# The score constant of each row as VectorE dot products, and y in two banks of 512

## The chip, the core and the metric

The kernel runs on one core of a Trainium2 chip. A core has five engines, each with a queue of its own that it works through in order: TensorE (PE in the profile; PEld is its loading of weights), VectorE (DVE), ScalarE (ACT), GpSimd (POOL) and SyncE (SP), which here issues transfers only. They wait for each other by semaphores. TensorE writes to eight accumulator banks (PSUM), which VectorE or ScalarE must empty. The metric is the device time of one execution in microseconds (us), the median of several runs.

## The reference, cut to what matters

```python
# x: (2708, 1024) f32, adj: (2708, 2708) of 0 and 1, sparse, the early rows dense
q, k, v = x @ W_q.T + b_q, x @ W_k.T + b_k, x @ W_v.T + b_v
z = (q @ k.T) / sqrt(1024) * adj
z = where(z == 0, -10000, z)
x = layernorm(x + relu(softmax(z, axis=1) @ v))      # layer 0
x = layernorm(x + adj @ (x @ weight) + bias)          # layer 1
```

Only the scores of a row's few neighbours matter. With M = W_q.T W_k and two vectors u and w (from the weights and biases), the score of row i and neighbour j is

```
z[i, j] = (y[i] . x[j]) / 32 + c[i],   y[i] = x[i] M + w,   c[i] = x[i] . u + (b_q . b_k) / 32
```

So the kernel computes y (1024 numbers a row) and the constant c (one number a row) once, keeps them in memory as one row of 1028, and gathers rows of y and x for each score. This change is about where c is computed.

## The kernel before, in words

The 2708 rows are 22 blocks of 128 (the last has 20). Rows are sorted by number of neighbours within two families, blocks 0 to 7 and blocks 8 to 21, so that each sorted block has a fixed number of neighbour slots (SLOTS, line 32).

*Start (to about 140 us).* The weights are loaded and turned, M is built (L608) and kept in four tiles m_sb of 1028 columns: 1024 of M, the column u (L601) and three of zeros. Beside it, `list_columns` reads the adjacency block by block and VectorE lists the neighbours (L222 to L229).

*y blocks.* `y_block(b)` (L289) multiplies a block of x, laid out as 8 tiles xt, with m_sb. Its 1028 columns are cut in three (y_cuts, L97: 342, 343, 343), each in one of the four banks of the pool p_o (L119), each over 8 products of 128 (L319). VectorE adds the bias row y_bc and moves each third to a tile yo (L323), with high priority in the schedule; SyncE stores yo (L328) to one of two arrays y_ds, one for each family. ScalarE sums the columns of xt meanwhile (`column_sums`, L332), for the mean row of x. Blocks 0 to 7 run in a loop of their own (L628), beside the rest of the listing, the dealing out of the densest rows (`deal_hub`) and the two sorts; `records_back(f)` (L585) turns the sorted records of a family, which GpSimd has scattered to memory and read back (tabs, L568), into degrees and masks; its first instruction is the copy at L593.

*Attention.* `attend(b)` (L788) gathers y for a sorted block (gather_y, L680, GpSimd's indirect transfers), gathers x rows for each slot into one of nine tiles g that are used in rotation (G1 = 9, L663; cleared once by GpSimd, L670), scores them on VectorE (L774), takes the softmax and adds up the weighted rows to r (L829 on ScalarE, L831 on VectorE). `attend_shares` does the same for block 0 and the hub rows (L908). A finished r is turned on TensorE (`flip`, L698) and multiplied with W_v (`project`, L721, two banks of p_o); VectorE empties these at L867.

*Order around the change.* A list written by hand, `steps` (L1042), says in which order y blocks 8 to 21, single projections ("v") and paired projections ("p") go to TensorE; a running credit (L1068) decides how many attention jobs are put beside each step. From this program order a scheduler makes the order of each engine's queue. Blocks 6 to 0 attend beside the second family's y; their y rows are of the first family. All other blocks gather y of the second family, so they begin when that is stored. What an instruction waits for holds up all that stands behind it on its engine.

*End.* After the paired projections of layer 0 (L958 in their shared code), layer 1 gathers sums of normalised rows and multiplies them with the second weight.

Of the kernel before, what the change touches and what calls it, by code (L numbers as in the profile page):

```python
# [9 lines left out]
F32 = mybir.dt.float32  # L10
# [5 lines left out]
ALU = mybir.AluOpType  # L16
# [4 lines left out]
P = 128  # L21
# [3 lines left out]
HALF = 512  # L25
# [17 lines left out]
ROW, DEG, OFF = 24, 25, 26  # L43
# [37 lines left out]
def sparse_part(ctx, tc, x, xT, adj, wqT, wkT, wvT, bq, bk, bv, w1, b1, out):  # L81
    nc = tc.nc
    N, D = x.shape
    DC = D // P
    NH = D // HALF
    scale = 1.0 / math.sqrt(D)
    NB = (N + P - 1) // P
# [6 lines left out]
    KW = HUB_KEYS + HUB_SLOTS + 5  # L94
    J0 = SLOTS[0]
    YW = D + 4
    y_cuts = [(YW * i // 3, YW * (i + 1) // 3) for i in range(3)]  # L97
    URGENT = 2000
    last = [b for b in range(NB) if SLOTS[b] == 0]
    single = [b for b in range(NB) if SLOTS[b] == 1]  # L100
# [11 lines left out]
    with es:  # L112
# [176 lines left out]
        def y_block(b):  # L289
            r0, n = b * P, rows[b]  # L290
            xt = xts[b]
            if b == NB - 1:
                column_sums(b)

                nc.vector.tensor_reduce(xbT, xs, AX.X, ALU.add)
                nc.vector.tensor_scalar_mul(xbT, xbT, 1.0 / N)
            yo = yos[b % 2]
            y_d, o0 = y_ds[b >= FAMILY], r0 - FAMILY * P * (b >= FAMILY)
            if b == NB - 1:

                assert n <= HUB
                po = p_o.tile([P, HALF], F32, name="po")
                with tc.high_priority(URGENT):
                    for c in range(DC):
                        for g in range(G):
                            nc.tensor.matmul(po[g * HUB:(g + 1) * HUB, :YW // G], xt[:, c, :HUB],
                                             m_sb[c // 2][:, c % 2, g * YW // G:(g + 1) * YW // G], start=(c == 0), stop=(c == DC - 1))
                    for g in range(G):
                        gs, cs = slice(g * HUB, g * HUB + n), slice(g * YW // G, (g + 1) * YW // G)
                        nc.vector.tensor_add(yo[gs, cs], po[gs, :YW // G], y_bc[gs, cs])  # L310
                for g in range(G):
                    gs, cs = slice(g * HUB, g * HUB + n), slice(g * YW // G, (g + 1) * YW // G)
                    nc.sync.dma_start(out=y_d[o0:o0 + n, cs], in_=yo[gs, cs])
                return
            firsts = []
            for h, (k0, k1) in enumerate(y_cuts):
                po = p_o.tile([P, HALF], F32, name="po")
                for c in range(DC):
                    put = nc.tensor.matmul(po[:, :k1 - k0], xt[:, c, :], m_sb[c // 2][:, c % 2, k0:k1], start=(c == 0), stop=(c == DC - 1))  # L319
                    if c == 0:  # L320
                        firsts.append(put)
                with tc.high_priority(URGENT):
                    nc.vector.tensor_add(yo[:n, k0:k1], po[:n, :k1 - k0], y_bc[:n, k0:k1])  # L323
            products.append(put)
            if b < NB - 1:
                column_sums(b, firsts)
            load_x()
            nc.sync.dma_start(out=y_d[o0:o0 + n], in_=yo[:n])  # L328

        def column_sums(b, behind=None):  # L330
            for c in range(DC):
                put = nc.scalar.activation(junka, xts[b][:, c, :], AF.Copy, accum_out=xs[:, c, b:b + 1])  # L332
                if behind is not None and c % 3 == 0:
                    follow(put, behind[c // 3])

        def follow(later, earlier, same=False):

            kind = mybir.DependencyClass.NoSync if same else mybir.DependencyClass.Sync
            tc.add_manual_dep(later.ins, earlier.ins.name, mybir.DependencyInfo(kind, mybir.DependencyReason.DATA),
                              reason="an engine's queue shall not stand still for a transfer")  # L340
# [241 lines left out]
            nc.vector.tensor_scalar(less_, ok, FAR, -FAR, op0=ALU.mult, op1=ALU.add)  # L582
            return put

        def records_back(f):  # L585
            b0, nb = families[f]
            bs, js = slice(b0, b0 + nb), slice(0, max(SLOTS[max(b0, 1):b0 + nb]))
            if f == 0:
                deg0 = lists.tile([P, 1], F32, name="deg0")
                follow(nc.vector.tensor_copy(deg0, tab0[:, DEG:DEG + 1]), products[-1])  # L590
                nc.vector.tensor_scalar_add(deg0[:HUB], deg0[:HUB], float(-J0))
                masks(valid0, less0, deg0)
            follow(nc.vector.tensor_copy(degs[:, bs], tabs[:, bs, DEG]), products[-1])  # L593
            masks(valid[:, bs, js], less[:, bs, js], degs[:, bs])


# [21 lines left out]
                    sorted_.append(0)  # L618
        y_bc = xa.tile([P, YW], F32, name="y_bc", bufs=1)
        bcast_rows(y_bc, y_col)  # L620
        mm = p_mm.tile([P, HALF], F32, name="mm")
        nc.tensor.matmul(mm[:, :1], ones, bqk, start=True, stop=True)
        nc.vector.memset(y_bc[:, D:], 0.0)
# [4 lines left out]
        for b in range(FAMILY):  # L628
# [17 lines left out]
                sort_end(1)  # L646
            if b == 0:
                records_back(0)
        records_back(1)
        wb.release()  # L650
        la.release()
        lists.release()
# [10 lines left out]
        def g_tile():  # L663

            return gp.tile([P, D], F32, name="g", tag="g")

        with tc.high_priority(URGENT):

            for _ in range(G1):
                nc.gpsimd.memset(g_tile(), 0.0)  # L670

        def gather(src, b, word, n):
            return gather_slot(src, tabs[:n, b, word:word + 1], n, g_tile())
# [348 lines left out]
        def finish_pair(pair, ts):  # L1022
            for k, (b, t) in enumerate(zip(pair, ts)):
                xr, sums = pair_x[b], [stat.tile([P, 1], F32, name=f"sm{h}", bufs=6) for h in range(NH)]
                for h in (0, 1) if k == 0 else (1, 0):
# [13 lines left out]
        late_jobs = [7, 20, 8, 19, 18, 8, 17, 8, 16, 11, 15, 10, 20, 9, 14, 19, 13, 12, 18]  # L1039
        late = set(late_jobs)  # L1040
        jobs, late_jobs = jobs + late_jobs, len(late_jobs)
        steps = [("y", 8), ("y", 9), ("y", 10), ("y", 11), ("v", 6), ("y", 12), ("v", 5), ("y", 13), ("v", 4), ("y", 14), ("v", 3),  # L1042
                 ("y", 15), ("v", 2), ("y", 16), ("y", 17), ("y", 18), ("y", 19), ("y", 20), ("y", 21)]
        steps += [("v", b) for b in [1, 0] + last] + [("p", pair) for pair in pairs]

        def blocks_of(step):
# [25 lines left out]
        for i, (kind, b) in enumerate(steps):  # L1072
            if pending is not None:
                pending[0](*pending[1:])
                credit -= END * (2 if pending[0] is finish_pair else 1)
                pending = None
            credit += STEP if kind != "p" else 2 * STEP - P_END
            step[0] = i
            for entry in joining[:]:
                if i >= entry[1] + 2:  # L1080
                    entry[1] = i
                    next(running[entry[0]])
                    if entry[0] in got:
                        joining.remove(entry)
            if kind == "p" and b == pairs[0]:

                (q11, q12), (q21, q22) = wv_q
                wv_t = differences()
                nc.vector.tensor_sub(q12, q12, q11)
                nc.vector.tensor_sub(wv_t[0], q22, q12)  # L1090
                nc.vector.tensor_sub(wv_t[1], wv_t[0], q11)
                nc.vector.tensor_sub(wv_t[2], q21, wv_t[0])
            for c in [c for st in steps[i:i + 3] for c in blocks_of(st) if not (left_y and c in late)]:
                while c not in done0 and c not in got and c != 0:
                    credit -= run_job()
            while 0 in jobs and i >= 15:
                credit -= run_job()
            while jobs and credit > 0 and len([c for c in got if c not in done0 and c not in ALONE and c != "hub"]) < (RB - 1 if left_y else RB):
                if left_y and len(jobs) <= late_jobs:
                    break  # L1100
                credit -= run_job()
            for k, c in steps[i:i + 2]:
                if k != "y" and c not in turned and not (left_y and k == "p"):
                    turned[c] = turn0(c) if k == "v" else turn_pair([lambda rT, r=got[b_]: flip(r, rT) for b_ in c], xb_pools[0])
                    done0.update(blocks_of((k, c)))
            if kind == "y":
                y_block(b)
                credit -= Y_END
                left_y -= 1
                if left_y == 0:  # L1110
                    xa.release()
                    xb_pool = tc.alloc_tile_pool(name="xb", bufs=1, side="right", reuse_waits="tile")
                    xb_pools.append(xb_pool)
                    xb_bc.append(xb_pool.tile([P, D], F32, name="xb_bc"))
                    bcast_rows(xb_bc[0], xbT)
            elif kind == "v":
                xr = gather_x(x, b)
                pending = finish0, b, (project_mean if b in last else project)(turned[b], wv_q), xr
            else:
                for b_ in b:  # L1120
                    pair_x[b_] = gather_x(x, b_)
                pending = finish_pair, b, project_pair(b, *turned[b])
# [460 lines left out]
```

## Time and profile before

The median is 1090.86 us of three runs (1090.35 to 1092.21).

| | busy us | share of the span |
|---|---|---|
| TensorE | 1015.2 | 93% |
| TensorE weight loads | 540.1 | 50% |
| VectorE | 826.3 | 76% |
| ScalarE | 428.1 | 39% |
| GpSimd | 486.7 | 45% |

| groups that the change touches | busy us | count | mean ns |
|---|---|---|---|
| L319 TensorE, y products of 342 and 343 columns | 296.3 | 1008 | 454 |
| L323 VectorE, evictions of y | 31.8 | 63 | 507 |
| L774 VectorE, scores of gathered rows (1024 wide) | 133.1 | 109 | 1221 |
| L721 TensorE, single projections (512 columns) | 101.7 | 224 | 611 |
| L867 VectorE, evictions of these | 10.8 | 16 | 683 |

How to read it: each f32 product of 128x128 is two records in the trace, so a y block of 24 products is 48. TensorE's records overlap: a mean of 454 ns is the time from the start of one to its own end, while the next starts earlier; the pace is read from start to start. Busy shares are over the whole span; what an engine costs in one stage has to be read from that stage.

### The profile page before, as it was taken

The page shows a single profiled execution, that of the slowest core. Times are in us where ns is not written, and L with a number is a line of the kernel's source. Part 1 is how long each engine was busy: PE and PEld are TensorE (multiplying, and loading weights), DVE is VectorE, ACT ScalarE, POOL GpSimd, SP SyncE. Part 2 cuts the span into 40 slices and gives each one's busy share as a digit, 9 for nine tenths or more (in the row PEclk, how much of TensorE's full clock was granted, in tenths as well). Part 3 has the DMA queues.
Part 4 walks back from the last instruction along what each step waited for, and adds up shares of the span by engine and source line. Part 5 has one row for each costly group of instructions (what it writes and reads, how often), then busy time and mean ns, then how long its engine had stood idle before and what let it go on. Part 6 is the DMA issues. An engine that isn't in the chain of part 4 may idle for free.

```text
span 1091.0 us, 10751 instructions
## 1 busy us (share of the span) xinstructions
PE 1015.2 (93%) x3177; PEld 540.1 (50%) x3177; DVE 826.3 (76%) x1801; ACT 428.1 (39%) x896; POOL 486.7 (45%) x397
## 2 busy tenths in 40 slices
PE   7999999999798989999998999999589999999993
PEld 6444466556454545466644444444244444445441
DVE  8799999980487789965297999984477777896431
ACT  4688697412131323232333253342512363324322
POOL 1000230067453546623066476631477777887300
PEclk9999999999999999999999899999799999999997
DMA  9555468435786746635142487835598689979601
GB/s 363 193 211 202 164 219 292 137 95 153 259 261 209 236 160 222 212 126 187 43 124 97 140 275 261 280 125 183 159 302 245 207 241 320 297 221 321 180 39 41
DMA packets 85219, 218.22 MB, mean 200 GB/s; under 512 B 15354, under 2 KB 37338, under 8 KB 82444
## 3 DMA queue, kind: packets, MB, share of 16 engines
q0 software_dynamic: 48768, 148.05, 42.3%
q1 hardware_dynamic: 36384, 69.40, 18.8%
q8 instruction: 27, 0.44, 0.2%
q14 instruction: 40, 0.33, 0.1%
HBM read 208.60 MB, written 33.68 MB: 222 GB/s over the span
## 4 chain that ended last, share of the span: by engine, by line
DVE 32%; PE 28%; issue 18%; DMA 10%; POOL 7%; ACT 3%; POOLq 0%; DVEq 0%; ACTq 0%
PE po L958 17%; PE po L319 6%; DVE few L225 6%; DVE a L222 5%; DVE junkv L774 5%; DMA g<-in_x_dram,tabs 4%; DVE r L831 3%; PE po L721 2%; POOL g L349 2%; DVE t L970 1%; POOL tab_d L563 1%; DMA g<-x_d,tabs 1%; DMA yg<-y_d,tabs 1%; PE tr L247 1%; POOL xr L343 1%
## 5 line engine op out<-in xcount | busy, mean ns | idle before, releaser
L319 PE MATMUL po<-m_sb,xt 128*128 128x343 f32 (+1 forms) x1008 | 296.3, 454 | 11.5 <-DVE yo L323 6.3
L319 PEld LDWEIGHTS po<-m_sb,xt 128*128 128x128 f32 x1008 | 190.4, 190 | 111.9 <-DVE yo L323 8.0
L774 DVE SCALAR_TENSOR_TENSOR junkv<-yg,g 128x1024 uint8<-128x1024 f32 x109 | 133.1, 1221 | 28.5 <-DMA g<-in_x_dram,tabs 16.2
L349 POOL DMA_INDIRECT g<-in_x_dram,tabs x86 | 114.3, 1330 | 76.4 <-ACT r L829 25.2
L958 PE MATMUL po<-t,s_all 128*128 128x512 f32 x272 | 126.6, 609 | 10.6 <-DVE t L970 6.5
L1191 DVE SCALAR_TENSOR_TENSOR r<-g,valid,r 128x1024 f32<-128x1024 f32 x77 | 98.6, 1281 | 17.8 <-DMA g<-x_d,tabs 17.2
L608 PE MATMUL po<-wk_o,wq_o 128*128 128x512 f32 x256 | 110.5, 592 | 0.0
L721 PE MATMUL po<-wv,rT 128*128 128x512 f32 x224 | 101.7, 611 | 6.2 <-DVE yo L323 2.8
L757 ACT ACTIVATE junks<-t,lnm 128x1024 uint8<-128x1024 f32 (+1 forms) x43 | 49.3, 1147 | 120.8 <-DVE lnm L755 103.9
L332 ACT ACTIVATE junka<-xt 128x128 f32<-128x128 f32 x176 | 53.9, 307 | 100.7 <-PE po L319 62.1
L958 PEld LDWEIGHTS po<-t,s_all 128*128 128x128 f32 x272 | 52.6, 196 | 78.2 <-issue 61.1
L958 PE MATMUL po<-w,rT 128*128 128x512 f32 x192 | 87.9, 607 | 0.0
L349 POOL DMA_INDIRECT g<-x_d,tabs x67 | 77.0, 1149 | 22.7 <-issue 16.5
L831 DVE SCALAR_TENSOR_TENSOR r<-g,pr,r 128x1024 f32<-128x1024 f32 x64 | 82.0, 1281 | 6.3 <-ACT r L843 4.8
L563 POOL DMA_INDIRECT tab_d<-rec,pos_i x22 | 25.1, 1141 | 129.9 <-DVE pos_i L552 123.5
L770 ACT ACTIVATE t<-t,nmr,rstd 128x1024 f32<-128x1024 f32 (+1 forms) x43 | 52.5, 1237 | 70.7 <-DVE nmr L769 64.2
L225 DVE MAX8 few<-a 128x8 f32<-128x75 f32 (+3 forms) x132 | 78.8, 616 | 0.0
L608 PEld LDWEIGHTS po<-wk_o,wq_o 128*128 128x128 f32 x256 | 48.4, 190 | 59.3 <-issue 59.0
L721 PEld LDWEIGHTS po<-wv,rT 128*128 128x128 f32 x224 | 43.2, 195 | 60.0 <-issue 53.5
L958 PE MATMUL po<-w,s_all 128*128 128x512 f32 x160 | 72.1, 592 | 0.0
L222 DVE SCALAR_TENSOR_TENSOR a<-a,iota 128x2708 f32<-128x2708 f32 (+1 forms) x22 | 65.2, 2963 | 5.4 <-ACT junk L221 5.4
L220 ACT ACTIVATE junk<-a 128x2708 uint8<-128x2708 f32 (+1 forms) x22 | 54.1, 2458 | 26.9 <-DMA a<-in_adj_dram 22.3
(332 smaller groups left out, 1475.4 us busy)
## 6 DMA issues: line engine op xcount, KB each, us to landing
a<-in_adj_dram SPq DMA_DIRECT2D x21, 1354.0 KB, 5.7
y_d<-yo SPq DMA_DIRECT2D x21, 514.0 KB, 5.4
xt<-in_xT_dram SPq DMA_DIRECT2D x21, 512.0 KB, 5.6
wq_i<-in_wqT_dram SPq DMA_DIRECT2D x8, 512.0 KB, 10.0
wk_i<-in_wkT_dram SPq DMA_DIRECT2D x8, 512.0 KB, 10.2
wv<-in_wvT_dram SPq DMA_DIRECT2D x16, 256.0 KB, 6.8
w<-in_w_dram SPq DMA_DIRECT2D x4, 1024.0 KB, 6.5
g<-in_x_dram,tabs POOLq DMA_INDIRECT x86, 5.6
```

The costliest lines, as they stand in the source:

```text
L220: nc.scalar.activation(junk[:n], a[:n], AF.Sign, accum_out=cnt[:n, b:b + 1])
L222: nc.vector.scalar_tensor_tensor(a[:n], a[:n], 1.0, iota[:n], op0=ALU.is_equal, op1=ALU.mult)
L225: nc.vector.max(few[:n, i * 8:(i + 1) * 8], a[:n, cuts[i]:cuts[i + 1]])
L319: put = nc.tensor.matmul(po[:, :k1 - k0], xt[:, c, :], m_sb[c // 2][:, c % 2, k0:k1], start=(c == 0), stop=(c == DC - 1))
L332: put = nc.scalar.activation(junka, xts[b][:, c, :], AF.Copy, accum_out=xs[:, c, b:b + 1])
L349: nc.gpsimd.indirect_dma_start(out=dst[:n], out_offset=None, in_=src, in_offset=bass.IndirectOffsetOnAxis(ap=at, axis=0), bounds_check=N - ...
L608: nc.tensor.matmul(po, wq_o[i // 2][:, o, i % 2 * P:(i % 2 + 1) * P], wk_o[:, o, hs], start=(o == 0), stop=(o == DC - 1))
L721: put = nc.tensor.matmul(acc, rT[:, c, :], w[c // 4][h][:, c % 4, :], start=(c == 0), stop=(c == DC - 1))
L774: nc.vector.scalar_tensor_tensor(junkv[:n], yg[:n, :D], scale, xg[:n], op0=ALU.mult, op1=ALU.mult, accum_out=s)
L831: nc.vector.scalar_tensor_tensor(r[:n], xg[j][:n], pr[:n, j:j + 1], r[:n], op0=ALU.mult, op1=ALU.add)
L958: put = nc.tensor.matmul(acc, a[:, k], w[:, k], start=start and k == 0, stop=stop and k == DC // 2 - 1, skip_group_check=True)
L1191: nc.vector.scalar_tensor_tensor(r[:n], xg[:n], ok[:n, j:j + 1], r[:n], op0=ALU.mult, op1=ALU.add)
```

## The change

The constant c leaves the product. y_block multiplies only the 1024 columns of M, in two banks of 512, and stores the first 1024 numbers of each row. The vector u is spread over all partitions once (u_bc). A new function, `row_constants(f)`, loads each block of x rows of a family into a g tile and takes the dot product with u_bc on VectorE, one instruction of 1024 a block, adds (b_q . b_k)/32, and stores four numbers a row (c and three zeros) into columns 1024 to 1027 of y_ds[f]. It is called for the first family after its y blocks, ahead of records_back(1), which is now ordered behind it on VectorE, and for the second family ahead of y block 17. The small block 21 keeps its old form, c included. In `steps`, each y block from 12 on moves ahead of the projection that it followed. column_sums is tied to four matmuls of a block instead of three.

The purpose is that a y block takes two accumulator banks of the four instead of three, and that the product has whole banks.

```diff
-    y_cuts = [(YW * i // 3, YW * (i + 1) // 3) for i in range(3)]
...
-            for h, (k0, k1) in enumerate(y_cuts):
+            for h in range(NH):
+                k0, k1 = h * HALF, (h + 1) * HALF
                 po = p_o.tile([P, HALF], F32, name="po")
                 for c in range(DC):
-                    put = nc.tensor.matmul(po[:, :k1 - k0], xt[:, c, :], m_sb[c // 2][:, c % 2, k0:k1], start=(c == 0), stop=(c == DC - 1))
-                    if c == 0:
+                    put = nc.tensor.matmul(po, xt[:, c, :], m_sb[c // 2][:, c % 2, k0:k1], start=(c == 0), stop=(c == DC - 1))
+                    if c % (DC // 2) == 0:
                         firsts.append(put)
                 with tc.high_priority(URGENT):
-                    nc.vector.tensor_add(yo[:n, k0:k1], po[:n, :k1 - k0], y_bc[:n, k0:k1])
+                    nc.vector.tensor_add(yo[:n, k0:k1], po[:n], y_bc[:n, k0:k1])
...
-            nc.sync.dma_start(out=y_d[o0:o0 + n], in_=yo[:n])
+            nc.sync.dma_start(out=y_d[o0:o0 + n, :D], in_=yo[:n, :D])
...
-                if behind is not None and c % 3 == 0:
-                    follow(put, behind[c // 3])
+                if behind is not None and c % 2 == 0:
+                    follow(put, behind[c // 2])
...
-        def records_back(f):
+        def records_back(f, behind=None):
...
-            follow(nc.vector.tensor_copy(degs[:, bs], tabs[:, bs, DEG]), products[-1])
+            put = nc.vector.tensor_copy(degs[:, bs], tabs[:, bs, DEG])
+            follow(put, products[-1] if behind is None else behind, same=behind is not None)
...
+        u_bc = xa.tile([P, D], F32, name="u_bc", bufs=1)
+        bcast_rows(u_bc, u_col)
...
-        records_back(1)
...
+        c_all = stat.tile([P, NB - 1, YW - D], F32, name="c_all", bufs=1)
+        nc.vector.memset(c_all, 0.0)
+        def row_constants(f):
+            b0, end = families[f][0], min(sum(families[f]), NB - 1)
+            for b in range(b0, end):
+                xg = g_tile()
+                nc.sync.dma_start(out=xg, in_=x[b * P:(b + 1) * P])
+                nc.vector.scalar_tensor_tensor(junkv, xg, 1.0, u_bc, op0=ALU.mult, op1=ALU.mult, accum_out=c_all[:, b, 0:1])
+            put = nc.vector.tensor_scalar(c_all[:, b0:end, 0], c_all[:, b0:end, 0], y_bc[:, D:D + 1], None, op0=ALU.add)
+            nc.sync.dma_start(out=y_ds[f][:(end - b0) * P, D:].rearrange("(b p) e -> p b e", p=P), in_=c_all[:, b0:end])
+            return put
+
+        put = row_constants(0)
+        records_back(1, put)
...
-        steps = [("y", 8), ("y", 9), ("y", 10), ("y", 11), ("v", 6), ("y", 12), ("v", 5), ("y", 13), ("v", 4), ("y", 14), ("v", 3),
-                 ("y", 15), ("v", 2), ("y", 16), ("y", 17), ("y", 18), ("y", 19), ("y", 20), ("y", 21)]
+        steps = [("y", 8), ("y", 9), ("y", 10), ("y", 11), ("y", 12), ("v", 6), ("y", 13), ("v", 5), ("y", 14), ("v", 4), ("y", 15), ("v", 3),
+                 ("y", 16), ("v", 2), ("y", 17), ("y", 18), ("y", 19), ("y", 20), ("y", 21)]
...
             if kind == "y":
+                if b == NB - 5:
+                    row_constants(1)
                 y_block(b)
```

## The prediction

> **What bounds the kernel now.** I read first the busy time per stage, then TensorE's idle stretches inside the stage that the change touches, then what VectorE did in those stretches. The stages are: the y blocks of the first family beside the listing of the adjacency (140 to 276.6 us), the y blocks of the second family beside the attention of blocks 6 to 0 (276.6 to 466.7), y blocks alone (to 540.3), the late attention jobs with the paired projections (to 730). Columns after the stretch: its length, then the busy time of TensorE, its weight loads, VectorE, ScalarE, GpSimd, then granted clock, DMA share, GB/s.
>
> ```profile
> 140.00:276.60 136.60, 132.39 (x466) 86.37 (x463) 103.56 (x309) 66.65 (x183) 50.39 (x54) 1.00 0.59 184
> 276.60:466.70 190.10, 172.41 (x522) 96.76 (x522) 157.27 (x281) 48.62 (x171) 97.53 (x75) 0.97 0.67 221
> 466.70:540.30 73.60, 73.60 (x312) 47.88 (x311) 34.73 (x72) 23.67 (x110) 15.58 (x13) 1.00 0.36 116
> 540.30:730.00 189.70, 182.08 (x596) 88.83 (x594) 173.88 (x371) 73.65 (x138) 109.16 (x77) 0.98 0.56 184
> ```
>
> TensorE is idle for 17.7 us of the second stretch and for nothing of the third, where VectorE has 39 us free. So the y stage ends when TensorE has done its work plus those 17.7 us. The idle stretches, and two rows that give the pace (start, duration, then idle before and its releaser in brackets):
>
> ```profile
> 280.86 11.19 PE L319 MATMUL po<-m_sb,xt 128*128 128x343 f32 x32 [4.23 <-DVE yo L323]
> 293.88 14.48 PE L319 MATMUL po<-m_sb,xt 128*128 128x342 f32 x48 [1.84 <-DVE nms L801]
> 320.50 4.88 PE L319 MATMUL po<-m_sb,xt 128*128 128x343 f32 x16 [2.03 <-DVE yo L323]
> 335.07 8.83 PE L721 MATMUL po<-wv,rT 128*128 128x512 f32 x16 [2.83 <-DVE yo L323]
> 385.78 4.88 PE L319 MATMUL po<-m_sb,xt 128*128 128x343 f32 x16 [3.29 <-DVE t L867]
> 451.16 15.67 PE L721 MATMUL po<-wv,rT 128*128 128x512 f32 x32 [2.56 <-DVE nm L892]
> ...
> 358.51 13.90 PE L721 MATMUL po<-wv,rT 128*128 128x512 f32 x32
> 372.24 1.04 PE L698 MATMUL tr<-ident,r 128*128 128x128 f32 x8
> ...
> 480.60 27.82 PE L319 MATMUL po<-m_sb,xt 128*128 128x342 f32 x96
> 508.26 0.28 PE L926 MATMUL mm<-den,tops 128*128 128x1 f32 x2
> ```
>
> Six waits, 16.8 us, all for VectorE to empty one of the four accumulator banks (the other 0.8 us waits for a transposed r). It is late not for lack of speed but of order: the eviction stands in its queue behind an instruction that waits for a transfer. The first case:
>
> ```profile
> 279.31 0.20 DVE L593 CAST degs<-tabs 128x14 f32<-128x14 int32 x1 [20.56 <-DMA tabs<-tab_d]
> 280.31 0.92 DVE L323 TENSOR_TENSOR yo<-po,y_bc 128x342 f32<-128x342 f32 x2
> 288.23 1.23 DVE L774 SCALAR_TENSOR_TENSOR junkv<-yg,g 128x1024 uint8<-128x1024 f32 x1 [7.00 <-DMA yg<-y_d,tabs]
> ```
>
> The attended rows r are not the limit: r of block 5 is done at 311.5 and turned on TensorE at 343.7. What follows the y stage does wait for it:
>
> ```profile
> POOL yg L343 <- DMA y_d<-yo: 35.7, 1, 35.7
> ```
>
> GpSimd stands for 35.7 us until the second family's y is stored, so the late jobs start when the y stage ends.
>
> **What the Trainium skill says.** "PSUM — Partial Sum Buffer", The four PSUM rules: a matmul's output fits one bank of 512 fp32. The trace has 343-column products, each taking a bank alone, and 512-column ones at L721; four banks hold 1371 columns of y now and 2048 after. "TensorE: Matmul & The Clock Gate", Back-to-back issue gap: the gap grows with the columns, plus about 2.5 ns. The trace agrees: 27.66 us / 96 = 288.1 ns for 342.7 columns, 13.73 / 32 = 429.1 ns for 512; that is 0.833 ns a column and a remainder of 2.6 ns. "Perfetto Trace Analysis", Per-engine timelines: ScalarE, VectorE and GpSimd are strict FIFO; the L593 line shows it. "DMA: Bandwidth & Descriptors", Anatomy of one DMA: about 2 us fixed, then bytes at 436 GB/s; that would be 3.2 us (estimate) for a 512 KB x tile, while the page of this kernel has 5.6 us for the 512 KB xt loads, and I use 5.6.
>
> **The change part by part.**
> *TensorE work.* A y block was 48 records of 288.1 ns = 13.83 us, and becomes 32 of 429.1 = 13.73: 0.10 us a block, 2.1 over 21. Eight transposes for u_bc add 1.0 (eight took 1.04 us at L191). Net 1 us: the narrower matrix is not what the change is worth.
> *VectorE work.* An eviction of 343 holds the engine 0.42 us to the next start, one of 512 0.60: 1.26 against 1.20 a block, nothing. Added are 21 dots of 1024; the like-formed L774 takes 1.25 from start to start: 26 us.
> *First family's dots (8).* They stand behind the found rows (250.5 us) and ahead of L593, in a stretch where VectorE is 0.66 us busy of 20 (260 to 280). The loads go out behind the store of y block 5 (229 us) as the g buffers are cleared (222 to 231); at 200 to 300 GB/s, 4.2 MB land by 245 to 252. Dots and c are done by about 263, c stored by 268, while yg is gathered at 281 because GpSimd issues one gather each 1.27 us until then. Hidden: 0. GpSimd has two x gathers fewer ahead of the last scatter, whose landing the read-back of tabs waits for (1.3 us each): L593 goes at 276.7 instead of 279.3.
> *Two banks instead of three.* Four banks were 18.4 us of lead for y blocks, now 27.5; with projections (two banks) alternating, about 22 becomes 27.5. Also y block 12 moves ahead of projection 6. I walk TensorE through the built kernel's own order. Block 7 ends at 258 as before; blocks 8 and 9 fill the banks until 285.7, after L593: the 4.23 us are gone. Bank 2 of block 8 is evicted after four scoring dots (288 + 6 = 294), so 10.2 waits 1.5 us, and blocks 11.1 and 11.2 some 2 us each in the same way: block 11 ends at 319. Then five times turn, y, projection at 0.87 + 13.73 + 13.73 = 28.33: 460.7. VectorE's evictions keep their places in its stream: projection 6 at 357, 5 at 385, 4 at 419, 3 at 450, where TensorE has these at 347, 376, 404, 432, never more than four banks ahead. So no further wait to 460.7, against 466.7 before, and y block 16 is inside it. Left are 17 to 20 and the small 21: 4 x 13.73 + 4 = 59: 519.7 if nothing holds it.
> *Second family's dots (13).* They stand between the evictions of 16.1 and 17.2, and add 16.3 us to VectorE's stream. The place that 16.2 takes in it came at 465.5 before (then bank 3 of block 15); with the dots and the adds of block 0 between, I count on from there and get 16.2 at 468, 17.1 at 489, 17.2 at 497, 18.1 at 505, 18.2 at 512. Block 20's banks are those of 18, so this is now as late as TensorE: end at 523. New waits come on top. Dots 5 to 9 load into g buffers that block 0's second piece reads only some 3 to 4 us earlier in the stream, against 5.6 to land: some 5 us. Nine tiles one after the other at 250 GB/s take 2.1 us each: some 2 more. The queue of SyncE has the store of c behind all dots, and behind that the xt of block 20: about 503 + 5.6 = 509, within the same delay. Bounds: 0 (all hidden) to 20 us (each of the nine late loads seen in full, 9 x 2.2). I take 5: the y stage ends at 528 instead of 540.2, 12.2 earlier.
> *After it.* The mean x (L295) now stands behind the last y eviction, where it was 1.3 us before the end; its path to the first L831 took 8.6 us (538.9 to 547.6), and 3 such adds came before the first scoring dot, while yg was in flight. I lose 2.5 of the gain. The rest (VectorE 92% busy to 730, then layer 1) shifts whole.
> Sum: 1090.9 - 12.2 + 2.5 = 1081.
>
> **The rivals.** *All hidden*: dot loads land in time and the mean costs nothing; end of y at 523, time 1090.9 - 17.5 = 1073. For it: 39 us of free VectorE in the third stretch. Against: the buffers reused within 4 us. *VectorE takes TensorE's place*: the delay is near 17 us, y ends at 540, and with the lost 2.5 the time is 1091 to 1093. For it: one queue for dots, evictions and block 0's adds. *Slower*: block 0's last piece has its gathers behind the dots' buffers, and the xt of block 20 behind c's store; 25 us of delay end y at 545 and give 1090.9 + 5 + 2.5 = 1098. Against: the DMA share there is 0.36.
>
> **How the numbers follow.** Forecast 0.52, all hidden 0.21, VectorE in place 0.14, slower 0.13. The range leaves out the slow case and the best of the hidden one: 1071 to 1092. Faster by over 0.2% (below 1088.7): the first two and a little of the third, 0.77; same 0.07; slower 0.16.
>
> **What would show it.** TensorE idle from 276 to 467 falls from 17.7 to under 8 us, with none before 285; L593 waits to about 277. Second-family dots (L682 there) show waits for their x loads of 3 to 8 us in all; y ends near 528. The first yg gather stays near 281. It is wrong if the c store or block 20's xt ends the stage, if an x load delays tabs, or if later stages take the shift back.

## The result, and the profile after

The changed kernel takes 1079.47 us (median of 4 runs, 1078.66 to 1080.41) against 1091.53 (4 runs, 1090.35 to 1093.06) for the kernel before: ratio 0.9889, 95% interval 0.9872 to 0.9906. On another chip it came out at 0.9889 again. The forecast of 1081 holds; its reason holds only in part, as the experiments show.

The busy time per stretch of the kernel after, columns as in the prediction (length, TensorE, its weight loads, VectorE, ScalarE, GpSimd, granted clock, DMA share, GB/s):

```profile
276.60:466.70 190.10, 183.98 (x456) 82.64 (x455) 157.73 (x271) 54.46 (x201) 94.60 (x72) 1.00 0.72 237
466.70:530.00 63.30, 61.47 (x239) 30.77 (x237) 45.66 (x94) 22.52 (x93) 23.54 (x19) 1.00 0.67 225
```

TensorE is idle for 6.1 us of the first stretch (17.7 before), and its granted clock there is 1.00 (0.97 before). TensorE's idle stretches in the kernel after, up to the end of the y stage (start, duration, form, then idle before and its releaser):

```profile
293.19 7.13 PE L319 MATMUL po<-m_sb,xt 128*128 128x512 f32 x16 [1.26 <-DVE yo L323]
301.28 7.13 PE L319 MATMUL po<-m_sb,xt 128*128 128x512 f32 x16 [0.95 <-DVE yo L323]
308.88 7.13 PE L319 MATMUL po<-m_sb,xt 128*128 128x512 f32 x16 [0.47 <-DVE yo L323]
317.54 14.14 PE L319 MATMUL po<-m_sb,xt 128*128 128x512 f32 x32 [0.65 <-DVE yo L323]
334.47 13.97 PE L739 MATMUL po<-wv,rT 128*128 128x512 f32 x32 [2.79 <-DVE pr L834]
...
512.42 3.67 PE L305 MATMUL po<-m_sb,xt 128*32 128x257 f32 x64 [1.29 <-DMA xt<-in_xT_dram]
```

The waits at 281, 386 and 451 us that the prediction showed have no successor. The VectorE lines that answer to the prediction's: the read-back of tabs, the first scoring dot, the only second-family dot that waited, and the last eviction of the y stage:

```profile
273.83 0.17 DVE L593 CAST degs<-tabs 128x14 f32<-128x14 int32 x1 [12.08 <-DMA tabs<-tab_d]
287.30 1.23 DVE L792 SCALAR_TENSOR_TENSOR junkv<-yg,g 128x1024 uint8<-128x1024 f32 x1 [11.84 <-DMA yg<-y_d,tabs]
471.62 1.22 DVE L682 SCALAR_TENSOR_TENSOR junkv<-g,u_bc 128x1024 uint8<-128x1024 f32 x1 [0.20 <-DMA g<-in_x_dram]
522.33 0.69 DVE L323 TENSOR_TENSOR yo<-po,y_bc 128x512 f32<-128x512 f32 x1 [4.38 <-PE po L319]
```

The y stage ends at 523.0 us (522.33 + 0.69) instead of 540.8: 17.8 us earlier. The profiled spans differ by 14.1 us only (1091.0 to 1076.9). So 3.7 us are given back later; the last experiments' section says where.

The 17.8 us are: 10.2 less of TensorE waits from y block 8 to the end of the y stage (17.6 to 7.4), 5.1 less lost to a halved clock there (5.1 to 0; summed as length times one minus the granted clock, in slices of 5 us), 1.3 less work (13 blocks at 0.10), and 0.6 by an earlier start of y block 8 (257.4 instead of 258.0). That leaves 0.6 unexplained. The clock term is not in the forecast at all, and part of it is luck: in a second profile of the same kernel it was 1.7 instead of 0.

### The profile page after: what moved, and what is told of

Its sections match the earlier page's. It is cut to its first block, busy times and chain, and to the rows that moved or that the text cites. A ratio compares the mean times of both kernels' runs of the same rounds, so it can differ in the third digit from the quotient of the medians.

```text
span 1076.9 us, 10217 instructions
## 1 busy us (share of the span) xinstructions
PE 1007.8 (94%) x2849; PEld 475.1 (44%) x2849; DVE 847.2 (79%) x1825; ACT 428.4 (40%) x898; POOL 490.7 (46%) x397
## 4 chain that ended last, share of the span: by engine, by line
PE 18%; issue 12%; DVE 11%; DMA 4%; POOL 3%; ACT 2%; POOLq 0%; DVEq 0%; ACTq 0%
PE po L976 16%; DVE junkv L792 2%; DVE r L849 2%; DMA g<-x_d,tabs 2%; DVE r L1211 1%; DMA yg<-y_d,tabs 1%; ACT junks L775 1%; DVE t L988 1%; POOL xr L343 1%; PE tr L716 1%; POOL g L349 1%; POOL x_d L703 1%; PE po L739 1%; PE tr L729 1%; POOL r L349 1%
## 5 line engine op out<-in xcount | busy, mean ns | idle before, releaser
L319 PE MATMUL po<-m_sb,xt 128*128 128x512 f32 x672 | 292.2, 594 | 3.3 <-DVE yo L323 3.3
L319 PEld LDWEIGHTS po<-m_sb,xt 128*128 128x128 f32 x672 | 126.4, 190 | 159.6 <-issue 150.8
L739 PE MATMUL po<-wv,rT 128*128 128x512 f32 x224 | 97.7, 594 | 3.3 <-DVE pr L834 2.8
```

The costliest lines, as they stand in the source:

```text
L319: put = nc.tensor.matmul(po, xt[:, c, :], m_sb[c // 2][:, c % 2, k0:k1], start=(c == 0), stop=(c == DC - 1))
L739: put = nc.tensor.matmul(acc, rT[:, c, :], w[c // 4][h][:, c % 4, :], start=(c == 0), stop=(c == DC - 1))
```

## Experiments

The theory after the result was the prediction's: two banks a block instead of three give VectorE more lead, so TensorE's waits go. The rivals were the four columns fewer, and the new order of steps, which the diff carries along.

**The old order of steps in the kernel after.**

```diff
-        steps = [("y", 8), ("y", 9), ("y", 10), ("y", 11), ("y", 12), ("v", 6), ("y", 13), ("v", 5), ("y", 14), ("v", 4), ("y", 15), ("v", 3),
-                 ("y", 16), ("v", 2), ("y", 17), ("y", 18), ("y", 19), ("y", 20), ("y", 21)]
+        steps = [("y", 8), ("y", 9), ("y", 10), ("y", 11), ("v", 6), ("y", 12), ("v", 5), ("y", 13), ("v", 4), ("y", 14), ("v", 3),
+                 ("y", 15), ("v", 2), ("y", 16), ("y", 17), ("y", 18), ("y", 19), ("y", 20), ("y", 21)]
```

> The kernel after with the old order of steps (projection 6 ahead of y block 12, and so on in turn). Bank-lead theory: two banks a block are what counts, the order is a small part; TensorE's waits for VectorE between 276 and 467 us stay below 10 us and the time is 1079 to 1083. Rival, the order of steps did it: the waits come back to 15 us or more and the time is 1086 to 1091.

Measured: 1093.65 us, ratio 1.0007 (0.9998 to 1.0016), above both expected ranges. With two banks and dots, but the old order, nothing is left of the gain. TensorE's waits in this kernel from block 8 on (total us, times, longest):

```profile
PE po L739 <- ACT rT L717: 10.1, 4, 6.1
PE po L319 <- DVE yo L323: 4.9, 4, 2.9
```

Before, 0.8 us of these waits were for the turned rows rT and the rest for evictions. Now 10.1 are for rT (9.5 of them before the end of the y stage). The lead let TensorE reach the projections earlier, where it found its operand missing: one wait took the place of another. The theory falls as the main cause.

**Three banks of 341 in the kernel after.**

```diff
-            for h in range(NH):
-                k0, k1 = h * HALF, (h + 1) * HALF
+            for k0, k1 in [(D * h // 3, D * (h + 1) // 3) for h in range(3)]:
```

> The kernel after with the 1024 columns of y in three banks (341, 341, 342) instead of two of 512: same TensorE work, same dots, same loads, same steps; only the lead of the four banks falls back from 27.5 to 18.3 us. Bank-lead theory: TensorE's waits for VectorE's evictions come back (12 us or more between 276 and 467), time 1086 to 1092. Rival, the four columns fewer and fewer, wider records did it: waits as in the kernel after, time 1079 to 1082.

Measured: 1082.09 us, ratio 0.9901 (0.9885 to 0.9916). Most of the gain is there without two banks. The waits did come back, as the bank theory says:

```profile
277.19 9.46 PE L318 MATMUL po<-m_sb,xt 128*128 128x341 f32 x32 [1.22 <-DVE yo L322]
293.84 24.64 PE L318 MATMUL po<-m_sb,xt 128*128 128x341 f32 x80 [7.20 <-DVE nms L818]
320.78 6.47 PE L318 MATMUL po<-m_sb,xt 128*128 128x342 f32 x16 [2.30 <-DVE yo L322]
```

but only up to 334 us; from there to the end at 530.0 TensorE never waits. So the two banks are worth the early part (the y stage ends 7 us earlier in after, 4 us in its second profile below), and the late part, 335 to 460, owes nothing to them. In the whole time the difference is 0.1%, inside the intervals.

**No dots.** The whole inner loop of `row_constants` is left out, so c lacks the dot product x . u.

```diff
-                xg = g_tile()
-                nc.sync.dma_start(out=xg, in_=x[b * P:(b + 1) * P])
-                nc.vector.scalar_tensor_tensor(junkv, xg, 1.0, u_bc, op0=ALU.mult, op1=ALU.mult, accum_out=c_all[:, b, 0:1])
```

> The kernel after without the 21 dots and the 21 x loads; the stored c is only the constant part, so the rows' dot products are left out. The trace of after shows 0.2 us of waits at the dots and the y stage's last eviction held by TensorE, so the dots are hidden: 1077.5 to 1080, no difference over 0.2%. Rival, my forecast's 5 us of delay by the dots: 1074 to 1075.

Measured: 1084.02 us, ratio 0.9912 (0.9895 to 0.993). Taking away 26 us of VectorE work and 11 MB of loads does not make the kernel faster; neither expectation had this. The read-back of tabs comes 3.6 us later than in after, and with it all of the early part:

```profile
277.40 0.18 DVE L593 CAST degs<-tabs 128x14 f32<-128x14 int32 x1 [24.74 <-DMA tabs<-tab_d]
```

GpSimd's queue shows why: without dots the g buffers are free early, and five x gathers stand ahead of the read-back (at 231, 249, 250, 269 and 271 us), at about 1.3 us each. In after the dots hold these buffers and one gather stands there (268).

**Three accumulator banks instead of four.**

```diff
-        p_o = es.enter_context(tc.tile_pool(name="p_o", bufs=4, space=PSUM))
-        p_tr = es.enter_context(tc.tile_pool(name="p_tr", bufs=3, space=PSUM))
+        p_o = es.enter_context(tc.tile_pool(name="p_o", bufs=3, space=PSUM))
+        p_tr = es.enter_context(tc.tile_pool(name="p_tr", bufs=4, space=PSUM))
```

> The kernel after with three accumulator banks instead of four (the bank goes to the transposes): lead 1.5 y blocks, 20.6 us, against 27.5 in after and 18.4 in before. Bank-lead theory: waits for evictions between 276 and 467 of 10 to 18 us, time 1084 to 1091. Rival, the form of the product did it: 1079 to 1081.

Measured: 1089.31 us, ratio 0.9962 (0.9949 to 0.9974). The time lies where the bank theory had it, but the waits don't: 9.4 us, all before 335 us, and the y stage ends at 530.6. This is no clean test of the lead either, since the read-back of tabs is passed at 277.7 us, 3.9 later than in after and as late as without dots, where the y stage ended at 529.1. Another 6 us came after the y stage: from there to the end of the span it takes 559.7 us against 553.9 in after. The cause of that stays open. The order of steps is thus the suspect; the next four runs, on one chip, are about it.

**The kernel after again.**

> The kernel after again, beside the next three on the same chip: ratio to before 0.987 to 0.991 in either theory.

Measured: 1080.91 us, ratio 0.9889 (0.987 to 0.9907). Its profile ends the y stage at 526.1 with 7.9 us of waits and 1.7 us of clock loss: two profiles of the same kernel differ by 3 us in this number.

**The new order alone, in the kernel before.** The two lines of `steps`, nothing else.

> The kernel before (three banks of 343, no dots) with only the new order of steps. Theory now, after the first four runs: the order is what counts, since a y block ahead of each projection gives the rows r and VectorE 13.7 us more; TensorE's idle time from 265 us to the y stage's end falls from 17.7 to about 12 and one or two of the three half-clock stretches go: 1080 to 1085. Rival, order and two banks are both needed (either alone only changes which wait it is): 1088 to 1092. Second rival, the dots' placement moves the read-back of tabs earlier and that starts it: also 1088 or more.

Measured: 1084.04 us, ratio 0.9915 (0.9896 to 0.9935). Two lines give three quarters of the whole change (0.85 of 1.11%). TensorE's waits in this kernel:

```profile
280.94 11.19 PE L319 MATMUL po<-m_sb,xt 128*128 128x343 f32 x32 [4.32 <-DVE yo L323]
293.75 19.11 PE L319 MATMUL po<-m_sb,xt 128*128 128x342 f32 x64 [1.62 <-DVE nms L801]
313.22 4.88 PE L319 MATMUL po<-m_sb,xt 128*128 128x343 f32 x16 [0.37 <-DVE nms L801]
321.36 6.57 PE L319 MATMUL po<-m_sb,xt 128*128 128x343 f32 x16 [3.26 <-DVE yo L323]
```

The early ones are much those of before (9.6 us against 8.1); the four at 335, 386, 420 and 451 us (9.5 us) are gone. VectorE shows why. The first three lines are of the kernel before, the next three of this one:

```profile
454.55 1.23 DVE L774 SCALAR_TENSOR_TENSOR junkv<-yg,g 128x1024 uint8<-128x1024 f32 x1
455.70 0.50 DVE L323 TENSOR_TENSOR yo<-po,y_bc 128x342 f32<-128x342 f32 x1
...
465.46 0.51 DVE L323 TENSOR_TENSOR yo<-po,y_bc 128x343 f32<-128x343 f32 x1
```

```profile
454.21 1.23 DVE L774 SCALAR_TENSOR_TENSOR junkv<-yg,g 128x1024 uint8<-128x1024 f32 x1
455.38 0.50 DVE L323 TENSOR_TENSOR yo<-po,y_bc 128x342 f32<-128x342 f32 x1
...
465.09 0.51 DVE L323 TENSOR_TENSOR yo<-po,y_bc 128x343 f32<-128x343 f32 x1
```

The same stretch of the scoring stream, at the same time within 0.4 us; but the evictions are of y block 15 before and of block 16 here. The table has the number of the 109 scoring dots that stand ahead of the last eviction of each y block in VectorE's queue, and the start of that eviction in us. (In the trace each dot is two records, the product and a read of its sum; they count once here. Which block an eviction belongs to follows from counting the evictions.)

```
y block   before       order alone   after, old order   after
12        30, 374.6    26, 352.1     30, 371.9          26, 350.3
13        40, 402.8    30, 373.2     40, 399.8          30, 372.3
14        50, 434.9    40, 403.1     50, 430.9          40, 400.7
15        60, 465.5    50, 434.4     58, 462.0          50, 432.8
```

VectorE's attention of blocks 6 to 0 keeps its own pace: dot 50 is passed by 431 to 435 us in all four. An eviction is tied to a place in it, not to a time. The new order moves each y block about one attention block (4 to 10 dots, 22 to 32 us) forward in that stream, whatever the bank count. So one y block more is done by the time the attention ends, and one less (13.7 us of TensorE) is left to do alone. That the order gives the gain is tested; that it does so by this place in the stream is read from the four traces.

**Three banks, dots, old order.** The edits of the first two experiments together.

> Three banks (341, 341, 342) with the dots and with the old order of steps: the kernel before in bank count and order, with only the dots and the four columns fewer. If the order is what counts: about as before, 1089 to 1094. If the old order harms only with two banks (TensorE reaches the projection before its rows r): 1082 to 1086.

Measured: 1097.68 us, ratio 1.0049 (1.0033 to 1.0066): slower than before, and than either expectation. Here the dots do cost: they stand ahead of evictions, and TensorE waits 22.0 us in all (17.6 before), 2.7 of it at 486 and 493 behind dots. The second family's dots themselves wait 4.5 us for their x loads here, and 6.2 in the kernel after with the old order, against 0.2 in after. The table of four by order and banks, all with dots (end of the y stage in us, ratio):

```
               old order        new order
three banks    544.1, 1.0049    530.0, 0.9901
two banks      537.4, 1.0007    523.0, 0.9889
```

The order is worth 1.2 to 1.5% in either row, and 0.85% without dots (the run before); the banks are worth 0.4% in the old order and 0.1% in the new one, where the intervals overlap. So in the old order two banks only win back what the dots cost (0.5%). What the order takes away differs by row: with three banks mostly waits for evictions, with two the 9.5 us of waits for rT, of which after has none before the end of the y stage. The four columns fewer fall as a cause: the run in the upper left has them and is slower than before.

**One more y block ahead of each projection.**

```diff
-        steps = [("y", 8), ("y", 9), ("y", 10), ("y", 11), ("y", 12), ("v", 6), ("y", 13), ("v", 5), ("y", 14), ("v", 4), ("y", 15), ("v", 3),
-                 ("y", 16), ("v", 2), ("y", 17), ("y", 18), ("y", 19), ("y", 20), ("y", 21)]
+        steps = [("y", 8), ("y", 9), ("y", 10), ("y", 11), ("y", 12), ("y", 13), ("v", 6), ("y", 14), ("v", 5), ("y", 15), ("v", 4), ("y", 16),
+                 ("v", 3), ("y", 17), ("v", 2), ("y", 18), ("y", 19), ("y", 20), ("y", 21)]
```

> The kernel after with every projection one more y block later (y block 13 ahead of projection 6, and so on). If TensorE's remaining idle time of 6 us is waiting for evictions of y blocks, more y blocks in a row don't help: 1079 to 1085. If a later projection still gains by rows that are surely ready: 1075 to 1078.

Measured: 1085.12 us, ratio 0.993 (0.9913 to 0.9948): worse than after. The wait moved to the end:

```profile
510.23 0.45 PE L934 MATMUL tr<-ident,nm 128*128 128x128 f32 x1 [6.70 <-DVE nm L913]
```

In after TensorE was already full from 335 to 511 us, and a second step has little to fill. The y stage ends at 531.6. But the edit moves more than y blocks: `row_constants(1)` goes with y block 17, so the 13 dots of the second family run at 405.9 to 434.1 us, inside the attention, instead of 460.9 to 486.0, and dot 40 is passed at 439 us instead of 400. How much of the loss is theirs was not tested.

The last four runs are of another chip, where the kernel before took 1107.37 us (1102.12 to 1115.05), so their ratios (0.9789 to 0.9876) are not set beside the others; what follows is read from the traces.

**No dots, with the read-back of tabs ahead of the x gathers.**

```diff
-            nc.gpsimd.indirect_dma_start(out=dst[:n], out_offset=None, in_=src,
+            put = nc.gpsimd.indirect_dma_start(out=dst[:n], out_offset=None, in_=src,
...
+            if len(held) < 8:
+                held.append(put)
+                follow(put, back[1], same=True)
...
-            nc.gpsimd.dma_start(out=tabs[:, bs, :], in_=tab_ds[f].rearrange("(b p) e -> p b e", p=P))
+            back[f] = nc.gpsimd.dma_start(out=tabs[:, bs, :], in_=tab_ds[f].rearrange("(b p) e -> p b e", p=P))
```

> The kernel after without dots and x loads (the rows' dot products are left out of c), as in the run without dots, but GpSimd issues the read-back of tabs ahead of the first eight x gathers, as the dots had brought about in after. If that place, and not VectorE, was why the run without dots came out slower than after: L593 back at about 272 instead of 277.4 us, y stage ends at 520 to 524, time 1075 to 1080. If the dots help in another way: the y stage ends near 529 again, 1083 to 1085.

Measured: 1084.07 us there. The read-back is passed at 274.5 instead of 277.4 us and the y stage ends at 525.3 instead of 529.1, about where after has it (523.0 and 526.1). This fits the place in GpSimd's queue as the cause of the loss without dots, but doesn't show it: 3.4 of these 3.8 us are half clock (5.1 to 1.7), two profiles of one kernel differ by 3 us, the time fell in the range of the other expectation, and the read-back came 2.5 us later than expected.

**The new order with the early read-back, three banks of 343, no dots.** The same edit in the kernel with the order alone.

> The kernel before with the new order of steps and with the read-back of tabs ahead of the x gathers; three banks of 343, no dots. If order and an early read-back are the gain and two banks are not needed: y stage ends at 522 to 527, 1076 to 1081, level with after or better. If two banks are needed for the rest: 1083 to 1085, as with the order alone.

Measured: 1086.2 us there. The read-back is early (275.7), the 4.32 us wait at 281 falls to 0.31, and the next one grows:

```profile
277.21 9.50 PE L319 MATMUL po<-m_sb,xt 128*128 128x343 f32 x32 [0.31 <-DVE yo L323]
294.87 5.48 PE L319 MATMUL po<-m_sb,xt 128*128 128x342 f32 x10 [8.16 <-DVE nms L806]
```

The y stage ends at 533.2, no better than with the order alone (530.4); 3.4 us of it is half clock that the order alone didn't have. With three banks the same blocks are held up a little later by the first scoring dots, which wait for yg to 289 us. Here two banks do their work: after has 1.26 us at this place.

**Five accumulator banks** (two for the transposes), in the kernel after and in the one of the last run.

> The kernel after with five accumulator banks (two for the transposes instead of three): lead 2.5 y blocks. If VectorE's pace through the attention sets where the evictions come, and the lead only moves the waits: TensorE's waits between 290 and 335 fall by at most the 7 us of one more bank, and the time is 1077 to 1084 with what the transposes lose. If lead is what counts: no waits, 1073 to 1077.

> As the kernel before with new order and early read-back, and with five accumulator banks (two for the transposes): lead 1.67 y blocks of three banks. If lead counts beside the order: 2 to 5 us below the same kernel with four banks; if not, no difference.

Measured: 1084.8 and 1095.08 us there; the second is 8.9 us slower than with four banks, where 2 to 5 faster or no difference was expected. Neither waits for an eviction between 290 and 335 us any more. But neither is a clean test: TensorE trickles through its products, to 270 us in the first and to 284 in the second, with pauses that in most cases nothing in the profile ends, the clock of the second is half from 254.7 to 288.8 us, and the first scoring dot comes at 298.4 and 304.1 us instead of 287.3. The second's profile is also of its slowest execution (1102.27 us). Two such lines of the kernel after with five banks:

```profile
265.04 0.59 PE L319 MATMUL po<-m_sb,xt 128*128 128x512 f32 x1 [0.81 <-issue]
269.97 56.41 PE L319 MATMUL po<-m_sb,xt 128*128 128x512 f32 x127 [1.79 <-issue]
```

Whether more lead than two banks of four helps is open. No version was shown to beat the kernel after.

**What is given back after the y stage.** From its end to the end of the span: 550.2 us before, 550.8, 551.0 and 551.1 in the three kernels of the first two chips with three banks of 341 or 343; 553.9 and 554.7 in after, 555.0 and 555.2 without dots and with the old order. VectorE's waits for yg in the 190 us from the end of the y stage on, before and then after:

```profile
DVE junkv L774 <- DMA yg<-y_d,tabs: 0.3, 1, 0.3
```

```profile
DVE junkv L792 <- DMA yg<-y_d,tabs: 4.8, 2, 2.9
```

In GpSimd's queue of before a yg gather stands between two stores of x_d (at 682.2, 683.6 and 685.5 us). In after both stores stand ahead of it (666.0, 667.5, then yg at 668.8), and VectorE waits for the yg that follows. It isn't the bank count as such: with one more y block ahead, two banks too, these waits are 1.6 us and the rest takes 550.7. No run changed this order by itself, so the 4.8 us of waits are a reading, not a test.

## Why the prediction was right, and where not

The time is right (1081 forecast, 1079.47 measured), and so are the bound (TensorE's waits behind VectorE's in-order queue), the small worth of the narrower matrix, and most of the walk: waits of 6.1 us in 276 to 467 against "under 8", none before 285, projection 2 done at 461.6 against 460.7, the first yg gather at 280.7 against 281.

The step that failed is "Two banks instead of three". It gave the lead of 27.5 us as the reason why no wait follows, and the moved y block 12 one sentence. The walk had the new order in it, so its number came out; its cause did not. The runs show that the order alone gives 0.9915, the banks and dots with the old order 1.0007. What the whole change gives beyond the order is 0.26%, and the intervals of the two overlap. None of the rivals named the order. The sentence "VectorE's evictions keep their places in its stream" held the answer: if a place is fixed to the attention's progress, moving a y block one attention block forward is the gain.

The terms of the sum:
- *Second family's dots.* Forecast 5 us of delay, y stage at 528. Measured 0.20 us of waits at the dots, end at 523.0 (526.1 in the other profile). The loads went out from 452.8 and 464.4 us on, early enough. In the old order the feared waits were there (4.5 and 6.2 us). The store of c (487.5) stood ahead of block 20's load of xt, but that load waited for its buffer to 489.6 anyway. TensorE waited for block 21's load only, 1.3 us, and that load had waited 13.9 us in SyncE's queue for GpSimd's clearing of its buffer, which no rival had.
- *The mean x behind the last eviction.* Forecast 2.5 us. From the end of the y stage to the first scoring dot it was 10.5 us before and is 10.7 after: 0.3.
- *First family's read-back.* Forecast 276.7, measured 273.8: four x gathers fewer stand ahead of the read-back, three of them ahead of the last scatter, where the forecast had two.
- *"The rest shifts whole."* It lost 3.7 us of the shift. Another order in GpSimd's queue is the reading of it, not tested.
- *The granted clock.* Not in the sum as a term. The walk ran after at 429.1 ns a record throughout, while the busy time of before had 5.1 us of half clock in it. That the walk came out is luck in this term: the profile of after had no half clock up to the end of the y stage, its second profile had 1.7 us.
- *Readings.* The 540.2 us for the end of the y stage before is the start of its last eviction; the stage ends at 540.8. Of the issue gap, only the remainder agrees with the section that the prediction cites: its formula has 1/2.4 = 0.417 ns a column, the records here take 0.833. And the estimate of 3.2 us for an x tile takes a fit for transfers that GpSimd issues; these go out from SyncE, and the measured 5.6 us was used.

In the profile the forecast is 5.6 us short on the gain of the y stage, 2.2 too high on the loss at the mean, and leaves out 3.4 that are given back elsewhere (3.7 less the 0.3 of the mean); these partly cancel, so part of the closeness of 1081 is luck.

## What to carry to other kernels

When two engines run in fixed orders side by side, ask at which place of the slower stream each hand-over stands before counting buffers; two lines of a hand-written order moved every hand-over by about a whole job. More buffers without that only changed which wait was seen. And when a diff carries an "and also" line, price it as a rival by itself.

## What the runs showed of the hardware

A short wait of TensorE can cost more than its length. In the kernel with three accumulator banks a wait of 2.10 us ends at 334.84:

```profile
334.84 8.83 PE L319 MATMUL po<-m_sb,xt 128*128 128x512 f32 x16 [2.10 <-DVE yo L323]
```

```profile
334.90:335.90 1.00, 1.00 (x2) 0.43 (x3) 1.00 (x1) 0.97 (x6) 0.10 (x1) 0.86 0.85 328
335.90:339.30 3.40, 3.40 (x6) 1.43 (x5) 2.14 (x7) 2.16 (x6) 0.00 (x0) 0.54 0.88 258
339.30:343.00 3.70, 3.70 (x10) 1.63 (x9) 3.54 (x3) 2.36 (x13) 2.93 (x2) 1.00 0.78 242
```

The clock (third number from the end) is near one half for 3.4 us, about 1 us after the wait's end, and the 16 records take 8.83 us instead of 7.13: 1.7 us on top of 2.1. In after a longer wait, 2.79 us, is followed by full clock (1.00 from 335.9 to 339.3). "TensorE: Matmul & The Clock Gate", Part 1, What's actually happening, says that the clock falls to half after an idle window of about 3.4 us, and that this window runs free of the work. The half clock and its 3.4 us agree, but the window need not be idle throughout, and the traces show what decides. In each of the fourteen, all changes of the clock lie on one fixed grid of 3.413 us, within 2 ns. Cut every wait of 1.9 us or more in the y stages at this grid: where one interval at full clock held 1.97 us (58%) of the wait or more, the next interval was at half clock; where no interval held more than 1.95 us (57%), it stayed full. The 2.10 us above lie in one interval; the 2.79 us in after are split into 1.27 and 1.52, and the 3.29 us before 385.78 in before into 1.71 and 1.58, so neither was followed by half clock. Where a wait falls on this grid is chance, and so is this part of what it costs.
